# First loads reordered, one product moved into the drain, and tokens 2p and 2p+1 to a partition, in a two-layer transformer kernel

## The chip, the cores and the metric

The kernel runs on one core of a Trainium2 chip. A core has five engines with instruction queues of their own: TensorE (PE in the profile, with its weight loads as PEld), VectorE (DVE), ScalarE (ACT), GpSimd (POOL) and SyncE (SP), which here issues nearly all DMAs. The metric is the device time of one launch in microseconds (us); less is better.

## The reference, cut to what matters

The input x is 16 sequences (batches) of 256 tokens by 256 features, in fp32. Four residual steps follow each other:

```python
x = x + attn0(cond(x, fside, fside, braak_embed[itok_5]))     # 16 heads of 16, causal, rotary
x = x + ffn0(cat_linear(x, W[itok_63], b[itok_63]))           # fp4-quantized gate, up, down
x = x + attn1(du_dt(x, zX, zY, zR))                           # 16 heads of 64, segments of 128
x = x + moe(partly_shared_mlp(x, experts[itok_15]))           # 8 experts, top 2, one shared
```

The first argument of `attn0` is itself an attention over `fside`, with one row of an embedding added to the queries. `du_dt`, which the change touches, is a reaction and diffusion step with reflecting borders, along the features and along the tokens:

```python
lap_x = y[:, :, left] - 2*y + y[:, :, right]     # neighbouring features
lap_y = y[:, up, :]   - 2*y + y[:, down, :]      # neighbouring tokens
du_dt = zX*lap_x + zY*lap_y + zR*y*(1 - y)
```

The fourth step first applies a 256 to 1024 layer with Gelu (`fc1`), then a 1024 to 192 layer that all sequences share (`fc2`) beside a 1024 to 64 layer chosen by the sequence; a router then sends each token to two of eight experts.

## The kernel before, in words

All products are fp32 on TensorE. In the trace each fp32 product is two MATMUL records, and each transpose (a product with the identity) one; the fillers are two.

The first stage, `woven`, does the first three steps for the 16 batches in a software pipeline. Eleven generators (`stage_a`, `stage_e`, `stage_gate`, `stage_up`, `stage_down`, `stage_f`, `stage_g`, `stage_p`, `stage_d`, `stage_v`, `stage_fill`) each yield one instruction at a time, or a condition to wait for. `weave` picks, while the program is built, the instruction that can start first by its own cost table, so the order on each engine is fixed in the program, by estimates in which every load takes 4.5 us. PSUM is split into two pairs of banks (`pair0`, `pair1`) and four `single` banks, handed out by the same list. All these instructions appear under one line (L162) in the profile.

`stage_a` loads batch 0 by `fetch_a`, then the weights of the first attention, and computes the cross attention and the heads' projections; `stage_gate`, `stage_up` and `stage_down` meanwhile load the feed-forward weights as `raw` tiles (`f_v` for the up matrix), quantize them and transpose them. `stage_fill` puts products of the identity on PE until the first batch has passed the first attention. `stage_e` finishes that attention, `stage_f` is the feed-forward step, `stage_p` loads the tables of the second attention and projects, `stage_d` calls `diffuse` (du_dt and the normalization), and `stage_g` and `stage_v` are the scores and the values of the second attention. `stage_v` ends each batch by storing x to a DRAM tensor `xd[b]`.

x is held as two tiles of 128 tokens: partition p holds tokens p and 128 + p. In `diffuse` the token neighbours come from a product with a 256 by 256 matrix `lap` (tridiagonal with the reflecting border), two products of K = 128 for each of the two token halves.

Near the end of the first stage, after the last batch has passed the feed-forward step, `stage_e` releases the memory of the first attention and calls `fetch_c`, which loads `x0` (batches 0 and 1 from `xd`), `fc1`, `fc2` and other weights of the fourth step ahead of it.

The second stage, `mixture`, begins with `conditioned`: for each of 8 blocks of 512 tokens it transposes x, multiplies by `fc1` with Gelu into `hT` (from a pool `k.hp` with two buffers), multiplies by `fc2` and by the chosen expert's matrix `own`, and routes. The shared expert and the tiles of the routed experts follow, then a gather that combines.

The queue of SP is served in order. `row_of` and `fetch_f` read an index of the batch from the tile `idx` on SP before they issue a load, so SP stands there until `idx` has landed.

Of the kernel before, what the change touches and what calls it, by code (L numbers as in the profile page):

```python
# [12 lines left out]
F32 = mybir.dt.float32  # L13
# [49 lines left out]
def setup(ctx, tc, a, n_batch):  # L63
    nc = tc.nc
    k = Ctx()
    k.nc, k.tc, k.a, k.B, k.turn, k.stream = nc, tc, a, n_batch, False, 0
    k.const = ctx.enter_context(tc.tile_pool(name="const", bufs=1))
    c = k.const
    k.ident = c.tile([P, P], F32, name="ident")
    make_identity(nc, k.ident)  # L70

    k.mask = c.tile([P, P], F32, name="mask")
    make_causal_mask(nc, k.mask, mask_val=NEG)


    idx = c.tile([64, 3, n_batch], I32, name="idx")
    for i, name in enumerate(("itok_B_0_5", "itok_B_0_63", "itok_B_0_15")):
        nc.sync.dma_start(out=idx[:, i, :], in_=a[name].unsqueeze(0).to_broadcast([64, n_batch]))
    k.idx = idx
    idxf = c.tile([64, 3, n_batch], F32, name="idxf")  # L80
    nc.vector.tensor_copy(idxf, idx)
    iota = c.tile([64, 1], F32, name="iota")
    nc.sync.dma_start(out=iota, in_=a["iota"])
    k.onehot = c.tile([64, 3, n_batch], F32, name="onehot")
    nc.vector.tensor_scalar(k.onehot, idxf, iota, None, ALU.is_equal)


    k.n_tiles = (TOPK * n_batch * S + NE * (TT - 1)) // TT
    dram = ctx.enter_context(tc.tile_pool(name="dram", bufs=1, space=bass.MemoryType.DRAM))
    k.ysort = dram.tile([NE * REGION * TT, D], F32, name="ysort")  # L90
    k.osort = dram.tile([k.n_tiles * TT, D], F32, name="osort")
    k.zero = c.tile([P, D], F32, name="zero")
    nc.gpsimd.memset(k.zero, 0.0)

    k.xd = [dram.tile([S, D], F32, name=f"xd{b}") for b in range(n_batch)]
    return k
# [198 lines left out]
def woven(k):  # L295
    nc, tc = k.nc, k.tc
    with ExitStack() as ctx:
        g = Stages()
        g.k, g.a, g.B, g.ident = k, k.a, k.B, k.ident
        g.pe, g.dve, g.act = Unit("PE", nc.tensor), Unit("DVE", nc.vector), Unit("ACT", nc.scalar)  # L300
        g.pool, g.sp = Unit("POOL", nc.gpsimd), Unit("SP", nc.sync)
        pool = lambda name, bufs, **kw: ctx.enter_context(tc.tile_pool(name=name, bufs=bufs, **kw))
        g.w = pool("w", 1)
        g.xp = pool("x", 5)
        g.f_, g.l_ = pool("sf", 1), pool("sl", 1)

        g.attention0 = tc.tile_pool(name="sa", bufs=1, side="right")
        g.a_ = g.attention0.__enter__()
        space = bass.MemoryType.PSUM
        psum = pool("psum", 1, space=space)  # L310
        g.pairs = [psum.tile([P, 2, 512], F32, name=f"pair{i}") for i in range(PAIRS)]
        g.singles = [psum.tile([P, 512], F32, name=f"single{i}") for i in range(8 - 2 * PAIRS)]
        g.zT = {}
        g.live, g.kT = {}, {}
        g.x, g.io, g.done = {}, {}, {"W": 0, "D": 0, "Z": 0, "A": 0, "M": 0, "E": 0, "F": 0, "P": 0, "G": 0, "V": 0, "L": 0}
        with tc.manual_schedule():
            weave([stage_a(g), stage_e(g), stage_gate(g), stage_up(g), stage_down(g), stage_f(g), stage_g(g), stage_p(g), stage_d(g), stage_v(g), stage_fill(g)])
# [41 lines left out]
def stage_a(g):  # L359
    k, a = g.k, g.a  # L360
    yield from fetch_a(g, 0)
    g.bout, op = load(g, g.w, "bout0", [P, D], a["L0_attn_b_out"].unsqueeze(0).to_broadcast([P, D]))
    yield op
# [4 lines left out]
    for name in ("cos0", "sin0", "nsin0"):  # L368
        t, op = load(g, g.w, name, [P, 2, DH0 // 2], a[name])
        setattr(g, name, t)  # L370
        yield op
    g.wout0, op = load(g, g.w, "wout0", [P, 2, D], a["w_out0"])
# [10 lines left out]
    for b in range(g.B):  # L383
        x = g.x[b]
        yield g.pool.tensor_tensor(x, x, g.bout.unsqueeze(1).to_broadcast([P, 2, D]), ALU.add)
        hT = yield from cross_attention(g, b)
        if b + 1 < g.B:
            yield lambda: b + 1 < g.done["L"] + 5
            yield from fetch_a(g, b + 1)
        yield lambda: g.done["A"] == b  # L390
        yield from project_heads(g, hT)
        for n in range(4):
            yield lambda: 4 * b + n < g.done["E"] + 2
            g.kT[4 * b + n] = yield from heads_maximum(g, n)
            g.done["M"] += 1


def stage_e(g):

    for b in range(g.B):  # L400
# [19 lines left out]
        yield copy_(g, oT, pt)  # L420
# [13 lines left out]
def fetch_c(g):  # L434

    k, a = g.k, g.a
    k.c2 = k.tc.tile_pool(name="c2_w", bufs=1, side="right")
    w = k.c2.__enter__()
    k.early = {}
# [12 lines left out]
    yield from get("fc2b", [P, 1], a["fc2_b"][0:P].unsqueeze(1))  # L452
    yield from get("wr", [P, 2, P + NE])
    yield g.sp.dma_start(out=k.early["wr"][:, :, P:], in_=a["w_router"])
    yield from get("expb", [16, 64], a["L1_cond2_experts_b"])
    yield from get("shared_b", [64, 1], a["fc2_b"][P : P + 64].unsqueeze(1))
# [3 lines left out]
    yield from get("bias2", [P, g.B])  # L460
    yield from get("xT0", [P, 2, 512])


def fetch_a(g, b):
# [9 lines left out]
    yield g.sp.dma_start(out=fT, in_=a["fT"][b])  # L474
    yield g.sp.dma_start(out=e, in_=row_of(g, a["L0_cond_braak_embed"], 0, b))
    yield g.sp.dma_start(out=f, in_=a["fside_BxSxS_0"][b].rearrange("(c p) d -> p c d", p=P))
    yield g.sp.dma_start(out=g.x[b], in_=a["x"][b].rearrange("(c p) d -> p c d", p=P))
# [173 lines left out]
def stage_f(g):  # L651
    k, a = g.k, g.a
    g.wc = {}
    yield from fetch_f(g, 0)
# [84 lines left out]
def quant_rows(g, name, dst, raw_tile, scratch):  # L739

    for r in range(0, FF0, 2 * P):
# [3 lines left out]
        for i in range(2):  # L745
            n = min(P, FF0 - r - i * P)
            yield g.sp.dma_start(out=raw[:n, i, :], in_=g.a[name][r + i * P : r + i * P + n, :])
        if both:
            flat = raw.rearrange("p i d -> p (i d)")
            yield from quantize(g, flat, flat, 2 * D, P, scratch)  # L750
        else:
            yield from quantize(g, raw[:, 0, :], raw[:, 0, :], D, P, scratch)
            yield from quantize(g, raw[:rows, 1, :], raw[:rows, 1, :], D, rows, scratch)
# [26 lines left out]
def stage_down(g):  # L780
# [3 lines left out]
    for r in range(2):  # L784
        raw = g.f_.tile([P, FF0], F32, name="raw", tag="d_h")
        yield g.sp.dma_start(out=raw, in_=g.a["L0_ffn_w_down"][r * P : (r + 1) * P, :])
        yield from quantize(g, raw, raw, FF0, P, scratch)
# [61 lines left out]
def stage_p(g):  # L849
    k, a = g.k, g.a  # L850
    yield lambda: g.done["A"] > 0 and g.done["W"] == 3
    g.lap, op = load(g, g.w, "lap", [P, 2, S], a["lap"])
    yield op
    g.z = []
    for n in ("condB_zX", "condB_zY", "condB_zR"):
        t, op = load(g, g.w, n, [P, g.B], a[n].unsqueeze(0).to_broadcast([P, g.B]))
        g.z.append(t)
        yield op
    g.gn, op = load(g, g.w, "g", [P, 2], a["g"])
# [61 lines left out]
def diffuse(g, b):  # L921

    zx, zy, zr = (z[:, b : b + 1] for z in g.z)
    y = g.x[b]
    one = yield from single(g, y)
    ply = one.rearrange("p (s d) -> p s d", s=2)
    for st in range(2):
        yield from mm_(g, ply[:, st, :], [(g.lap[:, c, st * P : (st + 1) * P], y[:, c, :]) for c in range(2)])
# [4 lines left out]
    yield g.dve.tensor_scalar(u, y, -1.0, 1.0, ALU.mult, ALU.add)  # L933
    yield g.dve.scalar_tensor_tensor(u, y, zr, u, ALU.mult, ALU.mult)
    yield g.dve.scalar_tensor_tensor(lx, y, -2.0, lx, ALU.mult, ALU.add)
# [16 lines left out]
    for c in range(2):  # L952
        yield g.act.activation(zT[:, c, :], pt[:, c, :], AF.Copy, scale=g.gn[:, c : c + 1])
# [49 lines left out]
def stage_v(g):  # L1003

    for i in range(4 * g.B):
# [4 lines left out]
        if n == 3:  # L1010
            yield g.sp.dma_start(out=g.k.xd[b].rearrange("(s p) d -> p s d", p=P), in_=g.x.pop(b))
            g.done["L"] = b + 1
# [37 lines left out]
def values4(g, n, b, prob, pm, v, wo):  # L1050
# [20 lines left out]
    yield copy_(g, oT, po)  # L1071
    g.singles.append(one)
    if n % 2 == 1:
# [5 lines left out]
        yield copy_(g, ppT, pt)  # L1079
# [16 lines left out]
def mixture(k, out):  # L1096
# [5 lines left out]
    with ExitStack() as ctx:  # L1102
# [6 lines left out]
        k.hp = ctx.enter_context(tc.tile_pool(name="moe_h", bufs=2))  # L1109
# [40 lines left out]
def shared_block(k, r, w1, w2, blk):  # L1150

    nc = k.nc
    hT = k.hp.tile([P, 8, 512], F32, name="hT", tag="hT")
# [250 lines left out]
def conditioned(k, keep, r):  # L1404
# [3 lines left out]
    with ExitStack() as ctx:  # L1408
        p2 = ctx.enter_context(tc.tile_pool(name="c2_p2", bufs=2))
        fc1, fc1b, fc2, fc2b, wr = (k.early[n] for n in ("fc1", "fc1b", "fc2", "fc2b", "wr"))  # L1410
        own = [k.early[f"own{i}"] for i in range(2)]

        nc.vector.tensor_copy(wr[:, :, 0:P], k.ident.unsqueeze(1).to_broadcast([P, 2, P]))

        bias2 = k.early["bias2"]
        nc.vector.tensor_copy(bias2[0:64, :], k.early["shared_b"].to_broadcast([64, B]))
        pb = bank(k)
        mm(nc, pb[64:128, :B], [(k.early["expb"], k.onehot[0:16, 2, :])])
        nc.vector.tensor_copy(bias2[64:128, :], pb[64:128, :B])

        for blk in range(NT // 4):
            k.stream = blk % 2
            for b in (2 * blk, 2 * blk + 1):
# [6 lines left out]
            xT = p2.tile([P, 2, 512], F32, name="g_xT", tag="g_xT", bufs=1) if blk % 2 else k.early["xT0"]  # L1430
            xs = k.xs[:, 4 * blk : 4 * blk + 4, :] if blk else k.early["x0"]
            transposed(
                k,
                xT.rearrange("p c (s t) -> p (c s) t", t=P),
                [xs[:, s, c * P : (c + 1) * P] for c in range(2) for s in range(4)],
            )
            x = k.xs[:, 4 * blk : 4 * blk + 4, :]
            nc.gpsimd.tensor_tensor(x, x, k.bs2.unsqueeze(1).to_broadcast([P, 4, D]), ALU.add)
            hT = k.hp.tile([P, 8, 512], F32, name="hT", tag="hT")
            for f in range(8):  # L1440
# [5 lines left out]
            nc.vector.tensor_scalar(k.yT[:, 0, blk * 512 : (blk + 1) * 512], py, fc2b, None, ALU.add)  # L1446
            for i in range(2):
# [22 lines left out]
def program(tc, a, out, n_batch):  # L1470
    with ExitStack() as ctx:
        k = setup(ctx, tc, a, n_batch)
        woven(k)
        mixture(k, out)

# [97 lines left out]
```

## Time and profile before

| | |
|---|---|
| median of 3 runs | 2772.08 us (2769.31 to 2772.41) |
| profiled execution, its own time | 2774.55 us |
| its span, first to last instruction | 2772.9 us |
| PE, PEld busy | 2692.8, 2039.9 us |
| DVE, ACT, POOL busy | 1434.2, 935.5, 858.2 us |
| mean granted TensorE clock | 0.983 |
| DMA | 270.65 MB, mean 98 GB/s |

Busy time is the union of an engine's instructions. In the page's strips the span is cut into 40 slices of 69 us; a digit is the busy share in tenths. A line of a timeline gives the start, the duration, the engine, the kernel's line, the operation and its tiles as out<-in, how many were merged, and in brackets the idle time before it and what ended it. A line of the stretches gives the busy time of PE, PEld, DVE, ACT and POOL with the number of instructions, then the granted clock, the busy share of the DMA engines and GB/s.

The first stage ends near 1795 us, where the last x is stored. The conditioned blocks reach to about 2070 us, the experts to 2657 us.

### The profile page before, as it was taken

What the parts mean: (1) busy time and instruction counts of PE and PEld (TensorE: products, weight loads), DVE (VectorE), ACT (ScalarE), POOL (GpSimd) and SP (SyncE); (2) the same over time, 40 slices, a digit from 0 to 9 for tenths busy, and PEclk for the clock granted to TensorE, in tenths of its full rate; (3) what the DMA queues carried; (4) which work ended last, traced back from release to release, by engine and by line L of the source; (5) the groups of instructions that cost most, each with busy time, mean ns of one, the idle gap of its engine ahead of it and who ended that gap; (6) DMA issues with size and microseconds to landing.
All of it is one profiled execution on the core that took longest, in us unless ns stands there. A gap on an engine that the chain in (4) does not pass through costs nothing. (4 is left out here: it accounts for less than half of the span.)

```text
span 2772.9 us, 42339 instructions
## 1 busy us (share of the span) xinstructions
PE 2692.8 (97%) x15999; PEld 2039.9 (74%) x15999; DVE 1434.2 (52%) x3113; ACT 935.5 (34%) x2418; POOL 858.2 (31%) x1030
## 2 busy tenths in 40 slices
PE   7999999999999999999999999899999999999999
PEld 6666777777777777777777778655566888888866
DVE  6556676776776776776776776433340000000023
ACT  2323334333333333333333334332222222222221
POOL 4323344434434334434434443323320000000035
PEclk7989999999999999999999999999999999999999
DMA  3222132222222222222322223131111455555523
GB/s 114 58 65 92 46 97 72 85 81 68 90 76 69 94 73 71 94 73 68 97 73 67 77 87 124 56 116 52 50 45 70 149 191 197 187 194 199 198 86 107
DMA packets 196030, 270.65 MB, mean 98 GB/s; under 512 B 33904, under 2 KB 166768, under 8 KB 186480
## 3 DMA queue, kind: packets, MB, share of 16 engines
q1 hardware_dynamic: 189680, 251.13, 28.2%
q0 software_dynamic: 6144, 16.79, 1.9%
q8 instruction: 128, 2.10, 0.3%
q14 instruction: 78, 0.64, 0.1%
HBM read 207.31 MB, written 60.56 MB: 97 GB/s over the span
## 5 line engine op out<-in xcount | busy, mean ns | idle before, releaser
L162 ACT ACTIVATE f_prob<-pair,f_stat 128x144 f32<-128x144 f32 x512 | 190.7, 378 | 225.8 <-DVE f_stat L162 172.0
L162 DVE TENSOR_TENSOR pair<-pair,mask 128x256 f32<-128x256 f32 (+1 forms) x384 | 198.5, 517 | 124.2 <-PE pair L162 92.8
L1228 POOL DMA_INDIRECT got<-osort,pos_o x64 | 62.0, 969 | 626.8 <-ACT hT L1161 586.3
L1210 ACT ACTIVATE ehT<-bank,own_b 128x256 f32<-128x256 f32 x280 | 132.8, 474 | 348.8 <-PE bank L49 348.8
L162 PE MATMUL single<-e_zT,wq 128*128 128x256 f32 x1024 | 249.6, 387 | 0.0
L49 PE MATMUL bank<-ysT,w 128*128 128x256 f32 x1120 | 247.6, 379 | 0.2 <-ACT ysT L113 0.2
L49 PE MATMUL bank<-w,ehT 128*128 128x256 f32 x1120 | 247.5, 379 | 0.0
L49 PEld LDWEIGHTS bank<-ysT,w 128*128 128x128 f32 x1120 | 212.7, 190 | 29.4 <-ACT ysT L113 0.5
L49 PEld LDWEIGHTS bank<-w,ehT 128*128 128x128 f32 x1120 | 210.2, 190 | 27.2
L162 PEld LDWEIGHTS single<-e_zT,wq 128*128 128x128 f32 x1024 | 186.8, 191 | 33.6 <-issue 4.5
L162 PE MATMUL pair<-keys,f_q 32*128 32x144 f32 x2048 | 159.8, 294 | 0.2 <-ACT f_prob L162 0.2
L162 ACT ACTIVATE b_e<-pair 128x768 f32<-128x768 f32 x128 | 103.7, 810 | 161.5 <-PE pair L162 151.4
L162 PEld LDWEIGHTS pair<-keys,f_q 32*128 32x128 f32 x2048 | 132.4, 184 | 27.7 <-issue 22.8
L162 POOL TENSOR_SCALAR_AFFINE_SELECT b_e<-b_e 128x512 f32<-128x512 f32 x128 | 83.9, 656 | 211.1 <-ACT b_e L162 210.3
L1218 DVE TENSOR_TENSOR eo<-bank,eb 128x512 f32<-128x512 f32 x35 | 24.2, 692 | 234.4 <-PE bank L49 227.8
L162 POOL TENSOR_TENSOR keys<-f_t,f_t 128x256 f32<-128x256 f32 x128 | 94.8, 754 | 150.9 <-DVE f_t L162 146.5
L162 PE MATMUL single<-wo,f_oT 128*128 128x256 f32 x512 | 131.9, 391 | 8.9 <-ACT f_oT L162 8.6
L162 DVE TENSOR_REDUCE qpad<-pair 128x2 f32<-128x256 f32 (+1 forms) x256 | 131.0, 554 | 4.4
L162 DVE TENSOR_TENSOR x<-x,single 128x512 f32<-128x512 f32 (+1 forms) x112 | 67.6, 604 | 121.2 <-PE single L162 121.1
L162 PE MATMUL pair<-b_qkT 16*128 16x128 f32 (+1 forms) x1024 | 123.3, 362 | 4.7 <-ACT b_qkT L162 3.3
L162 POOL TENSOR_TENSOR f_q<-f_t,f_t 128x256 f32<-128x256 f32 x128 | 93.5, 751 | 110.0 <-DVE f_t L162 109.7
L162 POOL TENSOR_TENSOR f_prob<-f_prob,f_stat 128x1024 f32<-128x1024 f32 x64 | 125.9, 1967 | 0.0
(300 smaller groups left out, 5240.0 us busy)
## 6 DMA issues: line engine op xcount, KB each, us to landing
w<-in_w SPq DMA_DIRECT2D x70, 1024.0 KB
ysort<-zero SPq DMA_DIRECT2D x32, 1024.0 KB
wq<-in_w_qk SPq DMA_DIRECT2D x128, 256.0 KB
wv<-in_w_v SPq DMA_DIRECT2D x64, 256.0 KB
wo<-in_w_out SPq DMA_DIRECT2D x64, 256.0 KB
ys<-ysort SPq DMA_DIRECT2D x35, 256.0 KB
osort<-eo SPq DMA_DIRECT2D x35, 256.0 KB
eb<-in_b SPq DMA_DIRECT2D x35, 128.0 KB
```

The lines of the kernel that those rows point to most:

```text
L49: nc.tensor.matmul(out, lhsT, rhs, start=start and i == 0, stop=stop and i == last)
L162: return Op([(self.name, self.cost(fn, outs, aps), lambda: call(*args, **kw))], outs, aps)
L1210: nc.scalar.activation(hT[:, f, :], ph, AF.Gelu_apprx_tanh, bias=b1[:, f : f + 1])
L1218: nc.vector.tensor_tensor(o, po, b2.unsqueeze(1).to_broadcast([P, 2, D]), ALU.add)
L1228: nc.gpsimd.indirect_dma_start(out=g, out_offset=None, in_=k.osort[:, :], in_offset=bass.IndirectOffsetOnAxis(ap=r.pos_o[:, i, t : t + 1], ...
```

## The change

Four things are changed together.

1. Loads. The three index loads leave `setup`; `fetch_a` issues them for batch 0 behind xT and fT and then lets SP wait until the first `raw` loads of the gate, up and down matrices have been issued (`done["R"] == 3`) before the embedding row, f and x. The bias `bout` is loaded behind the rotary tables, and added to x after the cross attention instead of before it. `stage_f` makes its first load after `wout0` has been issued. The one-hot of the third index (of 16 rows, in place of 64 rows of three) is made in `stage_p`.
2. Drain. A new stream `stage_c` starts when the last scores have been issued: it transposes x0 and does `fc1` and Gelu of block 0 into a tile `hT0` that is allocated by `fetch_c`. `conditioned` skips these for block 0. Even blocks keep `hT0`, odd blocks the one buffer left in `k.hp`. Small loads (`expb`, `fc2_b`) move from `fetch_c` to `conditioned`, and the bias product of the experts behind `fc2` of block 0.
3. Tokens. Partition p of x holds tokens 2p and 2p+1, so a load or a store of x is one run of 2 KB in each partition. Where a product's columns were in token order (`oT`, `f_oT`, `f_ppT`, `zT`), the copy out of PSUM now reads, or for `zT` writes, every second element.
4. Laplacian. With neighbours 2p and 2p+1 in one partition, the token neighbours of one parity are all in the other, so `diffuse` needs one product of K = 128 for each half, with a two-band matrix that POOL builds from the identity. The terms in y itself are folded into a factor: u = y*(zc - zR*y), zc = zR - 2*(zX + zY), which takes one VectorE instruction less.

The diff, cut to its core:

```diff
@@ setup
-    for i, name in enumerate(("itok_B_0_5", "itok_B_0_63", "itok_B_0_15")):
-        nc.sync.dma_start(out=idx[:, i, :], in_=a[name].unsqueeze(0).to_broadcast([64, n_batch]))
...
+    k.idx = c.tile([64, 3, n_batch], I32, name="idx")
+    k.onehot = c.tile([16, n_batch], F32, name="onehot")
@@ stage_a
     yield from fetch_a(g, 0)
-    g.bout, op = load(g, g.w, "bout0", [P, D], a["L0_attn_b_out"].unsqueeze(0).to_broadcast([P, D]))
-    yield op
...
+    g.bout, op = load(g, g.w, "bout0", [P, D], a["L0_attn_b_out"].unsqueeze(0).to_broadcast([P, D]))
+    yield op
     g.wout0, op = load(g, g.w, "wout0", [P, 2, D], a["w_out0"])
...
     for b in range(g.B):
+        hT = yield from cross_attention(g, b)
         x = g.x[b]
         yield g.pool.tensor_tensor(x, x, g.bout.unsqueeze(1).to_broadcast([P, 2, D]), ALU.add)
-        hT = yield from cross_attention(g, b)
@@ stage_e
-        yield copy_(g, oT, pt)
+        yield copy_(g, twined(oT), untwined(pt))
@@ fetch_c
+    k.h0 = k.tc.tile_pool(name="moe_h0", bufs=1, side="right")
+    hT0 = k.h0.__enter__().tile([P, 8, 512], F32, name="hT0")
...
+    g.done["C"] = 1
+
+def stage_c(g):
+    yield lambda: g.done["C"] and g.done["G"] == 4 * g.B
+    e = g.k.early
+    x, xT = e["x0"], e["xT0"]
+    for c in range(2):
+        one = yield from single(g, x)
+        pt = one.rearrange("p (s t) -> p s t", t=P)
+        for s in range(4):
+            yield g.pe.transpose(pt[:, s, :], x[:, s, c * P : (c + 1) * P], g.ident)
+        yield copy_(g, xT[:, c, :], one)
+        g.singles.append(one)
+    for f in range(8):
+        one = yield from single(g, xT)
+        yield from mm_(g, one, [(e["fc1"][:, c, f * P : (f + 1) * P], xT[:, c, :]) for c in range(2)])
+        yield g.act.activation(e["hT0"][:, f, :], one, AF.Gelu, bias=e["fc1b"][:, f : f + 1])
+        g.singles.append(one)
+
+def hidden(k, blk):
+    return k.early["hT0"] if blk % 2 == 0 else k.hp.tile([P, 8, 512], F32, name="hT", tag="hT")
+
+def untwined(t):
+    return t.rearrange("p c (t r) -> p c r t", r=2)
+
+def twined(t):
+    return t.rearrange("p c (r t) -> p c r t", r=2)
@@ fetch_a
     yield g.sp.dma_start(out=fT, in_=a["fT"][b])
+    if b == 0:
+        for i, name in enumerate(("itok_B_0_5", "itok_B_0_63", "itok_B_0_15")):
+            yield g.sp.dma_start(out=g.k.idx[:, i, :], in_=a[name].unsqueeze(0).to_broadcast([64, g.B]))
+        yield lambda: g.done["R"] == 3
     yield g.sp.dma_start(out=e, in_=row_of(g, a["L0_cond_braak_embed"], 0, b))
...
-    yield g.sp.dma_start(out=g.x[b], in_=a["x"][b].rearrange("(c p) d -> p c d", p=P))
+    yield g.sp.dma_start(out=g.x[b], in_=a["x"][b].rearrange("(p c) d -> p c d", p=P))
@@ stage_f
+    yield lambda: hasattr(g, "wout0")
     yield from fetch_f(g, 0)
@@ quant_rows, stage_down: behind the raw loads of a round
+        g.done["R"] += r == 0
@@ stage_p
-    g.lap, op = load(g, g.w, "lap", [P, 2, S], a["lap"])
-    yield op
+    g.lap, one = g.w.tile([P, 2, P], F32, name="lap"), g.ident
+    for r, dst, end in ((0, 1, 0), (1, 0, P - 1)):
+        cols = g.lap[:, r, dst : dst + P - 1]
+        yield g.pool.tensor_tensor(cols, one[:, 0 : P - 1], one[:, 1:P], ALU.add)
+        yield g.pool.tensor_tensor(g.lap[:, r, end : end + 1], one[:, end : end + 1], one[:, end : end + 1], ALU.add)
...
+    yield g.dve.tensor_tensor(zc, g.z[0], g.z[1], ALU.add)
+    yield g.dve.scalar_tensor_tensor(zc, zc, -2.0, g.z[2], ALU.mult, ALU.add)
+    yield g.dve.tensor_scalar(g.z[2], g.z[2], -1.0, None, ALU.mult)
@@ diffuse
     for st in range(2):
-        yield from mm_(g, ply[:, st, :], [(g.lap[:, c, st * P : (st + 1) * P], y[:, c, :]) for c in range(2)])
+        yield g.pe.matmul(ply[:, st, :], g.lap[:, st, :], y[:, 1 - st, :], start=True, stop=True)
...
-    yield g.dve.tensor_scalar(u, y, -1.0, 1.0, ALU.mult, ALU.add)
-    yield g.dve.scalar_tensor_tensor(u, y, zr, u, ALU.mult, ALU.mult)
-    yield g.dve.scalar_tensor_tensor(lx, y, -2.0, lx, ALU.mult, ALU.add)
+    yield g.dve.tensor_scalar(u, y, nzr, zc, ALU.mult, ALU.add)
+    yield g.dve.tensor_tensor(u, y, u, ALU.mult)
     yield g.dve.scalar_tensor_tensor(u, lx, zx, u, ALU.mult, ALU.add)
     yield g.dve.scalar_tensor_tensor(u, ply, zy, u, ALU.mult, ALU.add)
...
-        yield g.act.activation(zT[:, c, :], pt[:, c, :], AF.Copy, scale=g.gn[:, c : c + 1])
+        by_token = zT[:, c, :].rearrange("p (t r) -> p r t", r=2)
+        yield g.act.activation(by_token, pt[:, c, :].rearrange("p (r t) -> p r t", r=2), AF.Copy, scale=g.gn[:, c : c + 1])
@@ values4
-    yield copy_(g, oT, po)
+    yield copy_(g, twined(oT), untwined(po))
...
-        yield copy_(g, ppT, pt)
+        rows = lambda t: t.unsqueeze(1)
+        yield copy_(g, twined(rows(ppT)), untwined(rows(pt)))
@@ conditioned
+            hT = hidden(k, blk)
+            for f in range(8 if blk else 0):
```

## The prediction

> **What bounds the kernel now.** I read the page first, then the busy time by stretch, the groups of instructions, and the timelines of the two ends of the first stage.
>
> ```profile
> span 2772.9 us, 42339 instructions
> ...
> PE 2692.8 (97%) x15999; PEld 2039.9 (74%) x15999; DVE 1434.2 (52%) x3113; ACT 935.5 (34%) x2418; POOL 858.2 (31%) x1030
> ...
> PE   7999999999999999999999999899999999999999
> ...
> PEclk7989999999999999999999999999999999999999
> ```
>
> TensorE is busy 97% of the span; of the 40 slices only the first (7) and the 26th (8) are lower. So time is won by giving TensorE less work, or by filling those two holes. By stretch (PE, PEld, DVE, ACT and POOL busy, granted clock, DMA share, GB/s):
>
> ```profile
> 0.00:10.00 10.00, 7.96 (x52) 7.77 (x52) 0.63 (x2) 1.28 (x1) 4.30 (x14) 1.00 0.36 92
> 10.00:20.00 10.00, 2.84 (x7) 2.31 (x8) 0.98 (x3) 0.00 (x0) 2.48 (x2) 0.62 0.85 264
> 20.00:30.00 10.00, 6.42 (x36) 5.37 (x35) 9.76 (x19) 3.92 (x9) 6.62 (x8) 0.84 0.42 144
> 800.00:1200.00 400.00, 392.90 (x2813) 297.30 (x2810) 290.10 (x589) 157.78 (x454) 159.89 (x195) 1.00 0.25 79
> ```
>
> In the middle PE is idle 7.1 us of 400 and DVE is 73% busy. The first 10 us of PE are filler products; at 10 to 20 nothing computes while DMA moves 264 GB/s; at 20 to 30 DVE is full, with the quantization of the weights. The start in time order (start, duration, what, idle before and its releaser):
>
> ```profile
> 13.03 1.80 SPq L162 DMA_DIRECT2D raw<-in_L_ffn_w_gate  x2
> 14.62 1.26 POOL L162 TENSOR_TENSOR x<-x,bout 128x512 f32<-128x512 f32 x1 [9.54 <-DMA bout<-in_L_attn_b_out]
> 15.84 1.26 POOL L162 TENSOR_TENSOR a_qT<-xT,emb 128x512 f32<-128x512 f32 x1
> 17.16 3.78 PE L162 MATMUL pair<-fT,a_qT 128*128 128x256 f32 x8 [7.64 <-POOL a_qT L162]
> 18.95 0.69 DVE L162 TENSOR_REDUCE q_amax<-raw 128x32 f32<-128x512 f32 x1 [13.59 <-DMA raw<-in_L_ffn_w_gate]
> 23.65 0.68 DVE L162 TENSOR_REDUCE a_stat<-pair 128x2 f32<-128x512 f32 x1
> ```
>
> POOL waits for the bias `bout`, DVE for the first weight rows: both are late because they were issued late. The end of the first stage:
>
> ```profile
> 1777.72 1.99 PE L162 MATMUL single<-wo,f_oT 128*128 128x256 f32 x8
> ...
> 1782.83 1.90 POOL L162 TENSOR_TENSOR f_prob<-f_prob,f_stat 128x1024 f32<-128x1024 f32 x1
> ...
> 1784.78 1.97 PE L162 MATMUL single<-ident,f_prob 128*128 128x128 f32 x8 [5.06 <-POOL f_prob L162]
> ...
> 1797.23 14.00 PE L49 MATMUL bank<-xT,fc 128*128 128x512 f32 x32 [0.28 <-ACT xT L113]
> ...
> 1811.07 7.03 PE L49 MATMUL bank<-hT,fc 128*128 128x512 f32 x16
> ```
>
> PE stands 5.06 us behind the last softmax; the granted clock is then 0.50 from 1786 to 1794, so the last chain runs at half speed. The 14.00 us of `xT,fc` need nothing of that chain.
>
> **The change, part by part.** All durations are of the profiled execution: span 2772.9, its own time 2774.55, which is 2.5 above the median 2772.08. I take the differences off the median.
>
> Start. The program of the changed kernel has the same order on PE, DVE and ACT for the first 70 rows or so; only SP moves. It issues xT, fT, three idx, two raw gate, two f_v, raw down, then emb. Ahead of emb stand 256+256+12+256+256+352 KB. The DMA moved 190 to 260 GB/s in most stretches of this start and 362 at best, so with its own 128 KB emb needs 4 to 8 us from the first traffic, which comes about 1 us after the first issue at 0.8. Its own issue comes at about 6.5 (from 0.8 on: seven issues of 0.4, three of 0.6, and 0.8 for reading idx, as at 5.5 to 6.29 now). I estimate the landing at 10 (9 to 12). Then a_qT 1.26, no longer behind x+bout 1.26; scores 2.0 to 3.8 by the clock (1.99 in the middle of the run, 3.78 here); a_stat at about 15 instead of 23.65. The other way to a_stat: raw gate lands near 8, three rounds of amax, unit, reciprocal on DVE take 4.5, q_xn behind a_qT ends near 12.4, ACT 0.63, and q_big comes near 13.3: earlier. So -8.5; ends -4 (emb at 13 and a cold clock) and -10. Moved past on SP: the 1.5 MB now stand ahead of f, x, wqkv and bqkv. wqkv is then about 2.9 MB deep, landing at 11 to 15; it was first used at 33.41 and will be wanted at 25, so this is covered. bout now lands last and x+bout stands on POOL behind quantization work, wanted only at the residual sum at 98 us.
>
> Laplacian. 64 of 128 records `single<-x,lap` go. Eight of them take 1.83 us of PE from start to start (1081.91 to 1083.74), so four take 0.915; times 16 batches 14.6 us. PE is the bound in all but the first; I take -14. Ends: -15.25 (half of the group's 30.5 us busy) and -8, if the batches fall back on their chains. On DVE `lx-2y` (750 ns) goes and an 819 ns form becomes a plain product (nearest 604 to 690): 16 x 0.9 = 14 us off an engine that is 73% busy, counted at nothing. POOL builds the bands with four instructions (0.43 to 0.51 each by f_pm and e_lx), and DVE gets five of 0.2 near 98 us, where it idled 1.9 us before b_qk. They wait for zX, zY, zR and iota; if those land late, b_qk and the projection behind it wait. The lap load of 256 KB ahead of them is gone; 0, ends 0 and +2.
>
> Order of small products. Two 16 or 17 row groups that stand next to each other on PE save time: `b_qkT` and `b_qS` take 0.85 each alone, 1.51 together on the same rows (1059.11 to 1060.62), 0.88 together on other rows (1048.66 to 1049.54); so 0.2 or 0.83 saved. The program has 27 neighbours on other rows and 40 on the same before, 25 and 61 after (the keys groups behave alike, 1.18 alone): 30.4 against 33.0 us, -2.5; ends 0 and -4.
>
> x+bout behind the cross attention. PE waits 12.4 us for a_qT in 13 places, 7.6 of it at the start; the other 4.8 can fall by up to the 1.3 of x+bout each: -2, ends 0 and -4.8.
>
> Tokens 2p, 2p+1. Loads and stores of x become one run of 2 KB in place of two of 1 KB: DMA is at 0.25, 0. The copies f_oT (64), b_oT (16), f_ppT (32) read PSUM, and e_zT (32) writes SBUF, at every second element. No row shows that from PSUM; on SBUF the strided `b_t<-b_qk,sin` takes 432 ns against 415 for vpad, 4% more. I take 0 by that row; below 0 there is no reason. The upper end is doubled time for each element: ACT 586 for 512 and 373 for 256 gives 0.83 ns, so +0.43 and +0.21: 64x0.43 + 16x0.43 + 64x0.21 = 48 us on engines a third busy. PE waited for f_oT 13 times of 64, so about a quarter shows: +12.
>
> Drain. From 1779.7 the new order on PE is: x0 transposes 1.1, end 1780.8; xT copies behind the exps on ACT (1782.15) to 1783.35; fc1 0 in 1.75 to 1784.8; then f_prob, fc1 1, f_prob (1.1 and 1.75, end 1787.8, no 5 us hole, so no half clock), fc1 2, f_pT, fc1 3, f_pm, fc1 4 (5.25 and 1.4, end 1794.5), wo and pmo 2.9, fc1 5 to 7 in 5.25: 1802.6. The first bank then waits for the last Gelu of the old pool, 1.1: 1803.7 against 1811.07, -7.3. Behind the late x sum, SP stores xd and loads the rest of xs about 2 us later than now; block 1 wants them near 1819 and they land before 1810. Ends -4 (Gelus, behind one table load of 1.28, hold up the singles) and -9.
>
> Sum: -8.5 -14 -2.5 -2 -7.3 = -34.3; 2772.1 - 34.3 = 2738.
>
> [...]
>
> **The rivals.**
> Dear strided copies, which end on the other side. Place: f_oT, between values and output product, 64 times, and the three others. At double element time it decides against the change once 34.3 of the 48 us (71%) show on PE: at all of it 2738+48 = 2786, at a quarter 2750. For: PE already waits 8.6 us for f_oT. Against: 51 of 64 copies have slack, and SBUF's row is 4%. Chance 0.07, 0.03 of it slower. [...]
> Lost start. The early stretch fits no simple bound: clock 0.50 at 50 to 67, 132 to 152 and 190 to 203 us. If DVE and emb give only 4 and the half-clock stretches, 82 us before 310, grow by 8 (4 us of PE), 2738+4.5+4 = 2746 or so. Chance 0.15.
> Chains, not PE. Then the Laplacian gives 4 of 14 and the order 0: 2750. For: PEld is 74%, and a modelled PE can look full. Against: start to start of neighbours shows no gap. Chance 0.10.
> The change does not do what it says: the loads land no earlier, since the same bytes share the same engines (0 at the start), the Gelus of the drain hold up the singles and give back its 7.3, and the batches fall back on their chains. Then -4 from the Laplacian and -2 from POOL are left: 2766. For: DMA is already at 264 GB/s in the hole. Against: from 0 to 5 us it moves next to nothing. Chance 0.03.
>
> **How the numbers follow.** Forecast 0.65, 2738, own range 2726 to 2748. The range takes in the lost start, the chains and a quarter of dear copies, and downwards all best ends but one (-43, 2729) with clock stretches that vanish: 2723 to 2760. About 0.2% (5.5 us) is what a measurement here can tell from no change. Slower: 0.03 of the copies and 0.01 of the last rival. The same: 0.01 of the copies and 0.02 of the last. Faster: the rest, 0.93.
>
> **What would show it.** Right: a_stat near 15; 64 records of `x,lap` of the same length; no 5 us hole and no half clock at the drain; first `hT,fc` 7 us closer to the last f_prob product; f_oT at 586. Wrong: f_oT near 1000 and PE waits for it well over 8.6 us; a_qT still at 15; more time at half clock before 310 us; an idle PE in the middle above 7.1 us of 400.

## The result, and the profile after

| | before | changed |
|---|---|---|
| median of 16 runs | 2774.17 us (2769.31 to 2781.92) | 2765.66 us (2761.38 to 2773.94) |
| ratio | | 0.9966, 95% interval 0.9958 to 0.9974 |
| profiled span | 2772.9 us | 2767.1 us |
| PE, PEld busy | 2692.8, 2039.9 us | 2687.6, 2028.2 us |
| DVE, ACT, POOL busy | 1434.2, 935.5, 858.2 us | 1411.4, 945.9, 863.7 us |

The kernel became faster by 0.34%, some 9 us, where 34 were forecast. The page of the changed kernel, the lines that answer to those of before:

```profile
span 2767.1 us, 42187 instructions
...
PE 2687.6 (97%) x15929; PEld 2028.2 (73%) x15929; DVE 1411.4 (51%) x3061; ACT 945.9 (34%) x2457; POOL 863.7 (31%) x1034
...
PE   8999999999999999999999999999999999999999
...
PEclk7889999999999999999999999999999999999999
```

Both low slices of the PE strip have filled: the first went from 7 to 8, the 26th from 8 to 9. Yet PE is at 97% as before. By stretch, with the columns explained above:

```profile
10.00:20.00 10.00, 6.90 (x29) 6.18 (x30) 4.88 (x10) 2.96 (x7) 7.13 (x8) 0.66 0.89 310
20.00:30.00 10.00, 6.95 (x33) 4.49 (x32) 9.62 (x14) 2.82 (x6) 7.26 (x6) 1.00 0.33 109
800.00:1200.00 400.00, 391.05 (x2792) 294.47 (x2792) 282.25 (x569) 159.22 (x463) 162.25 (x195) 1.00 0.24 77
```

At 10 to 20 us PE now computes, and the DMA engines move 310 GB/s instead of 264. In the middle PE is *less* busy: 391.05 us of 400 against 392.90, so 9.0 us idle against 7.1, with 21 records fewer in the stretch. This is where the expected gain is missing, and the prediction had named it as a sign of being wrong (more than 7.1 us idle of 400). It is seen best in the distance between two batches, here two successive groups of the products with `lap` on PE, first of the kernel before, then of the changed one:

```profile
977.35 1.89 PE L162 MATMUL single<-x,lap 128*128 128x256 f32 x8
...
1081.91 1.89 PE L162 MATMUL single<-x,lap 128*128 128x256 f32 x8
```

```profile
972.46 1.13 PE L153 MATMUL single<-x,lap 128*128 128x256 f32 x4
...
1077.70 1.13 PE L153 MATMUL single<-x,lap 128*128 128x256 f32 x4
```

Half of the records are gone, as forecast, but the batch takes 105.24 us instead of 104.56. Measured over batches 4 to 12 (start of the first `lap` product of batch 12 less that of batch 4, by 8) the period is 104.55 before and 105.24 after. I use this number, the *period*, for every kernel below: kernels that have the same order and work agree in it within 0.05 us (105.24, 105.23, 105.23 and 105.28 for four), where whole runs of one kernel differ by 10. The period covers these eight batches alone; the first and the last batches have to be read beside it.

The drain, in order of time on PE of the changed kernel:

```profile
1778.35 1.99 PE L153 MATMUL single<-wo,f_oT 128*128 128x256 f32 x8
1780.18 1.04 PE L153 MATMUL single<-ident,x 128*128 128x128 f32 x8
1783.30 3.59 PE L153 MATMUL single<-xT,fc 128*128 128x512 f32 x4 [2.08 <-ACT xT L153]
1786.68 0.74 PE L153 MATMUL single<-ident,f_prob 128*128 128x128 f32 x4
...
1804.69 7.13 PE L49 MATMUL bank<-hT,fc 128*128 128x512 f32 x16 [0.78 <-ACT hT L153]
```

From the group `wo,f_oT` to the first product with `hT` it takes 26.34 us, before 33.35 (1777.72 to 1811.07). The 5.06 us hole has become one of 2.08.

### The profile page after: what moved, and what is told of

It reads as the page before. It is cut to its first block, busy times and chain, and to the rows that moved or that the text cites. A ratio compares the mean times of both kernels' runs of the same rounds, so it can differ in the third digit from the quotient of the medians.

```text
span 2767.1 us, 42187 instructions
## 1 busy us (share of the span) xinstructions
PE 2687.6 (97%) x15929; PEld 2028.2 (73%) x15929; DVE 1411.4 (51%) x3061; ACT 945.9 (34%) x2457; POOL 863.7 (31%) x1034
## 5 line engine op out<-in xcount | busy, mean ns | idle before, releaser
L153 PE MATMUL single<-wv,e_zT 128*128 128x256 f32 x512 | 124.4, 386 | 0.1
```

What stands on the lines that cost most here:

```text
L153: return Op([(self.name, self.cost(fn, outs, aps), lambda: call(*args, **kw))], outs, aps)
```

## The experiments

All times are medians of 4 to 12 runs, ratios are to the kernel before measured beside them. The medians were measured in several sets, in which the kernel before had 2772.8 to 2776.1, so a difference of two medians carries a doubt of some 3 us.

| kernel | what it is | us | ratio (95%) | period |
|---|---|---|---|---|
| old_list | new Laplacian and tokens, order of before | 2769.08 | 0.9990 (0.9977 to 1.0004) | 103.93 |
| rewoven | the same, order woven anew | 2775.64 | 1.0006 (0.9995 to 1.0017) | 104.16 |
| rewoven_bout | the same, x + bout moved | 2775.05 | 0.9995 (0.9985 to 1.0006) | 105.28 |
| loads_bout | the same, loads of the start moved | 2770.14 | 0.9980 (0.9969 to 0.9991) | 105.23 |
| changed_again | the same, new drain: the changed kernel | 2764.90 | 0.9968 (0.9956 to 0.9980) | 105.23 |
| after_bout_first | changed, x + bout back | 2764.61 | 0.9954 (0.9937 to 0.9971) | 104.17 |
| doubled | changed, lap products issued twice | 2769.23 | 0.9992 (0.9979 to 1.0005) | 105.29 |
| swapped | changed, two POOL instructions exchanged | 2757.83 | 0.9940 (0.9922 to 0.9958) | 104.19 |
| old_drain | old_list with the new drain | 2762.82 | 0.9947 (0.9927 to 0.9967) | 103.94 |
| spared | changed, order as if lap were unchanged | 2762.20 | 0.9945 (0.9922 to 0.9968) | 103.96 |
| hoisted | spared, first store of x later on SP | 2756.73 | 0.9928 (0.9910 to 0.9947) | 103.98 |
| hoisted2 | spared, second store of x later on SP | 2750.81 | 0.9904 (0.9887 to 0.9921) | 103.99 |

### The work and the order, taken apart

An edit that changes `weave`'s list reshuffles what stands behind it. To take the work away without that, an `Op` (one entry of the list) can keep its place and its cost in the list and issue something else, or nothing:

```diff
+def stands_for(op, *calls):
+    op.choices = [(name, cost, lambda: [c() for c in calls]) for name, cost, _ in op.choices]
+    return op
@@ diffuse, in the kernel before
-        yield from mm_(g, ply[:, st, :], [(g.lap[...], y[:, c, :]) for c in range(2)])
+        for c in range(2):
+            op = g.pe.matmul(ply[:, st, :], g.lap[...], y[:, c, :], start=c == 0, stop=c == 1)
+            real = lambda st=st: nc.tensor.matmul(ply[:, st, :], g.near[:, st, :], y[:, 1 - st, :], start=True, stop=True)
+            yield stands_for(op, *([real] if c == 0 else []))
```

> The kernel before with the new placement of tokens and the one-product Laplacian, but with the order of every instruction as it was before: the list still sees two products for each half and the third VectorE operation, and only one product and two operations are issued for them. Loads and drain are as before. Theory L (PE's work was worth what the prediction said; the newly woven order took it back): the batch period falls from 104.55 to 103.6 or 103.7 us, 16 batches give -12 to -14, total near 2760, ratio 0.995. Theory C (the waits hold the period whatever the order is, and PE only looks full): the period stays above 104.2, total within 5 us of before, ratio 0.998 or more.

> The same two parts put into the kernel before, with the order woven anew; loads and drain as before. Theory L: the period is 104.5 to 105.3 us, as in the changed kernel (105.24), total 2770 to 2785, that is 8 us or more above the kernel with the old order, though the work is the same. Theory C: within 3 us of the kernel with the old order.

> The changed kernel, whose list still sees a second product for each half of the Laplacian and a third VectorE operation that are not issued. Loads, drain and work are those of the changed kernel; only the order is another. Theory L: period 103.6 to 103.7, start -7 and drain -6.5 as measured, total 2745 to 2749, ratio 0.990 to 0.991. Theory C: the same as the changed kernel, 2762 to 2768, ratio 0.9966.

> The changed kernel in its own order, with each product of the Laplacian issued twice (the second repeats the first), 64 records more. Theory L (in any one order PE's work counts nearly in full): +10 to +14 us, total 2776 to 2780, ratio 1.0005 to 1.002. Theory C (in the new order waits are the bound and cover PE's work): +4 us at most, total 2766 to 2770, ratio 0.997 to 0.9985.

(The third VectorE operation is treated in the same way.) For `doubled` the edit only makes the call of the product twice.

Measured: in the old order the period falls to 103.93, by 0.62, between the two theories. The table of steps (start of each PE record to the start of the next, summed over a batch) shows it exactly: the products of the Laplacian go from 1.82 to 0.96, -0.86; nothing else changes but one group, `b_e,vpad`, which goes from 3.15 to 3.45, +0.30 (the rest is -0.06). So PE's work counts, less what the next wait takes back. The total lies where theory C put it: 4.5 us below before by the medians, and not clear of no change by the ratio. From the first `lap` product to that of batch 15 the trace gains 5.9 us where 15 times 0.62 would be 9.3; most of the rest goes at two holes that before doesn't have (1.96 us at 354.97 and 1.97 at 1600.85, last section).

The same work in the newly woven order gives 104.16, and 1757.6 instead of 1748.3 us at the first `wo,f_oT` product of the last batch: 9.3 us later in the two profiled executions, 6.6 by the medians, with more time at half clock (mean granted clock 0.981 in the profiled execution of rewoven, 0.983 in that of old_list). This is the way theory L points, but not its numbers (a period of 104.5 to 105.3, 8 us or more). `spared` shows that the period can be had back: 103.96. But its median stayed 13 us above its forecast, at the edge of theory C's range; a part of that has a cause of its own, below.

`doubled` is the sharpest: 64 products more move the period by 0.05. In the steps of a batch the Laplacian is at 1.83 again (+0.86), and `b_e,vpad` falls from 4.18 to 3.40 (-0.78). In the changed kernel's order the saved work had become waiting in front of that one group. The total is less clear than the period: +3.6 us by the medians, but 0.9992 against 0.9966 by the ratios, some 7 us, between the two theories. By the traces `doubled` is 3.0 us behind changed_again at batch 4 and 3.5 at batch 15, so it loses this ahead of the steady loop and next to nothing in it.

### Which edit chose the order

```diff
@@ stage_a, rewoven -> rewoven_bout; after_bout_first is the reverse in the changed kernel
-        yield g.pool.tensor_tensor(x, x, g.bout.unsqueeze(1).to_broadcast([P, 2, D]), ALU.add)
         hT = yield from cross_attention(g, b)
+        x = g.x[b]
+        yield g.pool.tensor_tensor(x, x, g.bout.unsqueeze(1).to_broadcast([P, 2, D]), ALU.add)
```

> The kernel rewoven (before, with the new tokens and the one-product Laplacian, order woven anew) and one thing more: x + bout stands behind the cross attention, as in the changed kernel. Same work, loads and drain as in rewoven. Theory O (the place of that one POOL instruction sends the planner onto another order, and the order sets the batch period): the period is that of the changed kernel, 105.2 us, against 104.16 in rewoven, +9.5 us over nine batches, of which the two last batches give back some 6; total 2775 to 2782. Theory P (the period of the changed kernel comes from the loads or the drain, or from the freed POOL time): the period stays at 104.2, or falls by the up to 1.3 us that a_qT waited.

> The changed kernel with x + bout put back ahead of the cross attention; everything else, the load of bout behind the rotary tables too, as changed. Theory O: the period is that of rewoven, 104.16 instead of 105.24, 9 batches -9.7; the two last batches take some 7 more, as in rewoven; a_qT of batch 0 now waits for the late bout, +2 or +3 at the start: total within 4 us of the changed kernel, 2762 to 2770, with the period as the mark. Theory P: the period stays at 105.2.

Measured: 105.28 with the addition behind the cross attention, 104.17 with it ahead, whatever loads and drain do. Theory O holds for the period: the place of one instruction of 1.27 us on POOL, which was counted as a gain of 2 us, chose an order whose batch is 1.1 us longer. In after_bout_first the start falls back as well (a_stat at 24.4 us instead of 16.9), further than the 2 or 3 us expected. The totals of rewoven and rewoven_bout agree all the same (2775.64 and 2775.05), because that order is 10 us ahead at batch 4 (first `lap` product at 550.8 against 560.8) and quicker over the last two batches (169.9 against 176.9 us from batch 13 to 15).

### What holds PE in that order

POOL and PE of the changed kernel at one place in a batch:

```profile
976.14 0.85 POOL L153 TENSOR_TENSOR f_pm<-f_prob,f_stat 128x128 f32<-128x128 f32 x1
976.95 1.89 POOL L153 TENSOR_TENSOR f_prob<-f_prob,f_stat 128x1024 f32<-128x1024 f32 x1
...
978.44 0.63 PE L153 MATMUL single<-b_e,vpad 128*32 128x256 f32 x4
978.80 0.63 POOL L153 TENSOR_SCALAR_AFFINE_SELECT b_e<-b_e 128x512 f32<-128x512 f32 x1
...
979.49 0.84 PE L153 MATMUL single<-b_e,vpad 128*32 128x256 f32 x12 [0.42 <-POOL b_e L153]
```

PE has issued four of the 16 products `b_e,vpad` and stands for the select of the rest of `b_e`, which waits on POOL behind 1.89 us of `f_prob`. The group takes 1.82 us from start to start instead of 0.79. The gap in the record shows only 0.42 of the 1.03, because the records of the four products before it reach into the wait. The next kernel only exchanges the two on POOL:

```diff
@@ weave, where an instruction is issued
+        if held and engine == "POOL" and out.startswith("b_e"):
+            call()                       # the select first
+            return held.pop()[1]()       # then the multiplication of f_prob
...
+        if engine == "POOL" and out.startswith("f_prob") and "f_stat" in names(op.ins)[-1]:
+            held.append((out, call))
+        else:
+            call()
```

> The changed kernel with one exchange on POOL, twice in a batch: where the multiplication of f_prob (1.9 us) stands directly ahead of a select of b_e, the select goes first. PE, VectorE and ScalarE keep their order, and no work is added or taken. In the changed kernel the first of these places holds the 16 products b_e,vpad for 1.03 us a batch, 0.42 of it shown as a gap. Theory W (that wait is on the path that sets the period): the period falls from 105.24 to 104.2 to 104.6, total -6 to -9, near 2757. Theory M (the wait is only where the slack of another path becomes visible, and it moves): f_prob, now 0.65 later, holds its transposes instead, the period stays above 105.0, total within 2 us.

The same place in this kernel:

```profile
968.84 0.63 POOL L153 TENSOR_SCALAR_AFFINE_SELECT b_e<-b_e 128x512 f32<-128x512 f32 x1
969.44 1.89 POOL L153 TENSOR_TENSOR f_prob<-f_prob,f_stat 128x1024 f32<-128x1024 f32 x1
...
970.35 0.86 PE L153 MATMUL single<-b_e,vpad 128*32 128x256 f32 x16
```

All 16 products run in one go, the period is 104.19, -1.05, and in the steps of a batch `b_e,vpad` falls by 1.03 while no other group moves by more than 0.02. Theory W holds: this wait was on the path. The total falls to 2757.83, ratio 0.9940 against the changed kernel's 0.9966 and 0.9968, so 7 to 8 us (5 to 6.5 if each median is taken less that of before beside it).

The same table closes the account of the period from before to changed, +0.69: the Laplacian's products -0.85, `b_e,vpad` +1.03 (3.15 to 4.18), all other groups together +0.51. In the kernel before this group takes the same 3.15 as in swapped, so the wait was not there. It came in two parts: with the products of the Laplacian doubled the new order has 3.40, and the other 0.78 came as that work was taken away. So the new order costs 0.74 us a batch at the old work (104.55 to 105.29), and in it the saving is worth 0.05.

### The start and the drain

loads_bout is the changed kernel without the drain's part (`stage_c`, `hT0` and the moved small loads); its PE, DVE, ACT and POOL have the order of rewoven_bout up to the last scores, but for two small VectorE instructions that the one-hot needs.

> The changed kernel without the new drain: same order on PE, VectorE, ScalarE and POOL as in rewoven_bout and the changed kernel up to the last scores; against rewoven_bout only the loads of the start differ. Theory S (the start is worth its 7 us, but a half-clock stretch between 46 and 80 us, which comes in two lengths, takes it back in some executions): a_stat near 17, the first product with lap 7 us earlier than in rewoven_bout (near 171) where that stretch is short and about as early (179) where it is 20 us long; median -3 to -7 against rewoven_bout's 2775, that is 2768 to 2772. Rival (the start's gain is lost behind the next wait in every execution): 2775 and the first product with lap at 179 with a short stretch too.

> The changed kernel once more, on the chip of loads_bout. Against loads_bout only the drain differs: -6 to -7 us if the drain keeps what it gained in old_drain, -3 or less if not. The ratio to the kernel before stays within 0.995 to 0.998.

> old_list (the new Laplacian and tokens in the order of before) and the new drain: block 0's first product in the list behind the last scores, nothing else. Theory D (the drain is worth what the prediction says, whatever the rest): everything up to 1745 us as in old_list, the first product with hT 7 us earlier, no half-clock stretch of 10 us behind it, total -6 to -7 against old_list, near 2762. If the gain at the drain needs the other parts: -3 or less.

Measured, start: a_stat (the first reduction of the cross attention's scores) at 18.0 instead of 23.4 us, the first `lap` product at 171.3 instead of 178.5, ratio 0.9980 against 0.9995: theory S. In the profiled execution of the changed kernel the lead of 6.5 us at a_stat was gone by the a_stat of batch 1, at 81.4 us against 80.5 in rewoven_bout. The changed kernel, and then changed_again, by stretch:

```profile
50.00:60.00 10.00, 9.38 (x60) 7.82 (x58) 8.62 (x22) 2.81 (x5) 4.66 (x8) 0.65 0.01 2
60.00:70.00 10.00, 10.00 (x58) 6.82 (x54) 6.41 (x13) 2.02 (x5) 3.17 (x4) 0.50 0.00 0
70.00:80.00 10.00, 10.00 (x70) 8.07 (x69) 4.28 (x9) 4.12 (x9) 3.86 (x4) 0.67 0.01 2
```

```profile
50.00:60.00 10.00, 9.30 (x56) 7.74 (x56) 7.90 (x20) 2.92 (x6) 4.61 (x9) 0.66 0.01 2
60.00:70.00 10.00, 9.87 (x102) 7.60 (x106) 7.93 (x19) 4.83 (x11) 5.24 (x7) 1.00 0.01 2
70.00:80.00 10.00, 9.54 (x92) 7.23 (x85) 5.68 (x13) 4.66 (x13) 3.19 (x5) 1.00 0.15 40
```

The same program in the same order: at 60 to 70 us it is granted 0.50 in one execution and issues 58 records, and 1.00 in the other and issues 102. The half-clock stretch lasts 20.5 us in the first (from 53.0) and 6.8 in the second; the first `lap` product comes at 179.5 and at 172.2. What the loads gain is as large as what this stretch takes or leaves, and the two are not quite separated: of the 7.2 us by which loads_bout leads at the first `lap` product, 4.3 are left from batch 3 on, and it also has 10.2 us less at half clock before 310 us than rewoven_bout (68.3 against 78.5), which at half speed would be worth 5.

Measured, drain: `old_drain` has its first product with `hT` 5.1 us earlier than old_list, though its last batch was 1.8 us later: -6.9 from there, and medians -6.3. In the changed order, changed_again against loads_bout, the medians give -5.2, and the time from the `wo,f_oT` group to the first product with `hT`, read as in the first section, falls from 31.2 to 26.3. By the ratios the drain would be worth 12 us in the old order (0.9947 against 0.9990) and 3.3 in the new (0.9968 against 0.9980); with intervals of 3 to 6 us each, these scatter by as much as is to be measured. By medians and traces it is worth 5 to 7 us in both orders.

### A load behind a store

`spared` lost a part of its forecast at one place. PE and SP there:

```profile
479.74 0.33 SPq L153 DMA_DIRECT2D xd<-x  x1
...
484.02 1.21 SPq L153 DMA_DIRECT2D wq<-in_w_qk  x2
...
489.65 2.93 PE L153 MATMUL single<-e_zT,wq 128*128 128x256 f32 x6 [5.10 <-DMA wq<-in_w_qk]
```

SP stood from 459.9 to 479.7 for x, which the store `xd` writes out; `wq` was issued behind it, and PE idled 5.10 us. The clock was at 0.50 for 6.8 us behind that.

```diff
@@ weave, on SP alone, at one store of x
+        if engine == "SP" and not done and (held or out.startswith("xd1")):   # hoisted: xd0
+            if out[:2] in ("wq", "wv"):                                       # hoisted: wo too
+                call()                                # the weights at once
+                if out[:2] == "wv": done.append(1); [h() for h in held]
+            else: held.append(call)                   # the store and the loads behind it
```

> spared, with one stretch of SP's queue in another order: the first store of x and the loads of batch 5 stand behind the weights (wq, wo, wv) of the next head group instead of ahead of them. In spared PE stood 5.1 us at 484 us for wq, whose load stood behind that store on SP, and a half-clock stretch of 6.8 us followed. Theory H (the late load and the clock cost 5.1 + 3.4): the hole goes, no half clock at 489, total -8 against spared's profiled 2762, near 2754. Rival: the wait moves to batch 5's x or to the store and the total stays within 2 us.

> spared with the swap on SP's queue at the right place: the second store of x, the loads of batch 6 and wo stand behind wq and wv of the next head group. (hoisted made it at the first store, where PE does not wait.) Theory H: the hole of about 5 us at 481 to 490 us and the half clock behind it go, -6 to -8 against hoisted (median 2756.7), near 2750, ratio 0.990 to 0.991. Rival: wq is still late, or a later load takes its place: -2 or less.

Measured: `hoisted` was a miss. I had taken the store of batch 0, and the hole is at that of batch 1: it stayed (4.8 us at 481), and the 5 us in the median go with a shorter half-clock stretch at the start (from 54.3 us 6.8 us long in its profiled execution, from 52.1 us 23.9 long in that of spared), not with the exchange: two of the five runs of spared took 2754.55 and 2755.89, as short as hoisted's. `hoisted2` exchanges at the right store: no gap over 1.5 us between the holes at 355 and 1599, median 2750.81, ratio 0.9904. It is the fastest kernel here, -6 against hoisted as theory H has it; and the profiled executions of spared and hoisted2, which have the same 85.3 us of half clock before 310 us, take 2762.4 and 2755.0. Exchanging the POOL pair in it as well was not tried.

## Why the prediction was wrong

The sum by its own steps, with what the chain rewoven_bout, loads_bout, changed_again gives (ratios times 2775, each with an interval of some 3 us to either side, so that the single rows are rough):

| step | predicted | measured |
|---|---|---|
| start | -8.5 (-4 to -10) | -4.2; by the trace -7.2 at the first `lap` product, -4.3 from batch 3 on |
| Laplacian | -14 (-8 to -15.25) | |
| order of small products | -2.5 (0 to -4) | |
| x + bout | -2 (0 to -4.8) | the three together -1.4 |
| copies | 0 (0 to +12) | 0 |
| drain | -7.3 (-4 to -9) | -3.3; by the traces -4.9 (from loads_bout) to -7.0 (from before) |
| sum | -34.3 | -8.9 |

**The step that failed** is the Laplacian, in its first sentence: "PE is the bound in all but the first". PE was busy 97% and start to start showed no gap between neighbours, so I took each record off PE as its price in time. The work did leave as forecast: 64 records, and 0.85 us a batch by the steps, 13.7 in 16. But a price in time needs more: that the other engines keep PE fed when it needs 0.9 us less, and that the new order is as good as the old. Neither held. Where the order stays, 0.62 of 0.86 us arrive and 0.30 come back as waiting at `b_e,vpad` (old_list), and the total gains 4.5 us by the medians, short of the -8 at which my range for this term ended. Where the order is woven anew, the period falls by 0.39 (rewoven) or rises by 0.73 (rewoven_bout), and in the changed kernel's order the work is worth 0.05 in the period (doubled): a wait for POOL, nearly hidden between overlapping records, is on the path, and swapped takes it away and gets all of it.

The order as a whole was treated as a by-product worth -2.5, counted by neighbours of the same row groups. That count was near: by the steps the three groups (`b_qkT`, `b_qS,b_qkT`, `keys,f_q`) take 0.20 us a batch less, 3.2 in 16. What it left out was larger, and of either sign: at equal work the period is 103.93, 104.16 or 105.28. The sentence on x + bout failed with it: the wait for a_qT did go (12.4 us in 13 places before, 4.4 in one place after, at the start), but the instruction's new place chose another order.

Of the rivals, "Chains, not PE" (0.10) named the mechanism, but gave 4 of 14 and 0 for the order, so 2750; that the order can cost as much as the work saves was in no case, and so the range ended at 2760. The last rival (0.03) gave 2766, the number that came, but by luck: it had the start and the drain give nothing, and both gave. PE's busy share hardly tells the slower order from the faster one: from 800 to 1200 us it is 391.05 us in the changed kernel and 392.03 in swapped. In the one group that differs, 1.03 us of waiting showed as a gap of 0.42, so the records in front of it looked longer than their work.

**Start.** Right in mechanism: emb let a_qT go at 11.79 instead of behind bout at 15.84, a_stat came at 16.9 (predicted 15), the first reduction of the weights on DVE (`q_amax`) at 6.54 instead of 18.95. What the whole run keeps of it goes with the half-clock stretches, as the rival "Lost start" had it: before 310 us they are 82 us in before, and 85 and 68 in two executions of the changed kernel.

**Drain.** Right, and nearest in size: the order on PE is the one written down, 5 to 7 us by the traces. The first fc1 product came at 1783.30 (worked out: 1783.35), but behind its hole of 2.08 us the clock was half for 3.4 us, so it took 3.59 us and not 1.75, and the first `hT,fc` came at 1804.7 (worked out: 1803.7).

**Copies.** Right. The copy of `f_oT` out of PSUM, all of it contiguous before and at every second element after, and `e_zT`, which is written so (least, median and greatest duration in ns):

```profile
L162 ACT COPY f_oT<-single x59: 567/586/596, 278.1 to 1789.2; 128x512 f32<-128x512 f32 x59
L162 DVE COPY f_oT<-single x5: 684/692/692, 362.5 to 1776.7; 128x512 f32<-128x512 f32 x5
...
L162 ACT ACTIVATE e_zT<-single,g x32: 467/474/485, 211.3 to 1676.8; 128x256 f32<-128x256 f32 x32
```

```profile
L153 ACT COPY f_oT<-single x50: 582/586/591, 276.6 to 1792.4; 128x512 f32<-128x512 f32 x50
L153 DVE COPY f_oT<-single x14: 691/692/692, 471.8 to 1777.3; 128x512 f32<-128x512 f32 x14
...
L153 ACT ACTIVATE e_zT<-single,g x32: 478/496/513, 208.0 to 1677.6; 128x256 f32<-128x256 f32 x32
```

586 ns on ACT and 692 on DVE, as before; the write costs 5% more (496 ns against 474). The rival with the dear copies fell: no run shows the doubled element time from which it and the upper end of +12 were reckoned, and for these reads by ACT and DVE the measurement shows no price.

## What to carry to other kernels

In a kernel whose order a planner writes, an edit's price has two parts, the work and the new order; hold the order (an entry that stands for the old one) to see the first alone, and compare periods of the steady loop, which repeat to 0.05 us where runs scatter by 10 (the first and the last batches still need the total: rewoven and rewoven_bout differ by 1.1 us in the period and by 0.6 in the median). A TensorE at 97% did not say here that its work was the time (64 products more moved the period by 0.05 us): issue the products in question twice, and if the period does not move, look at the steps from start to start for the group that waits. There one exchange of two instructions on an engine that is a third busy was worth nearly as much as the whole change.

## What the runs showed of the hardware that was not expected

Short holes cost more than themselves in these runs. Behind a hole of about 2 us on PE the granted clock was 0.50 for 3.4 us in 18 of 34 cases, which at half speed would cost another 1.7 (an estimate: half of 3.4; at the drain of the changed kernel four records `xT,fc` behind such a hole took 3.59 us, and the next four, at 1787.26, 1.88). In old_list, a product behind such a hole, and then the stretch of time that it begins, with the granted clock in the third column from the right:

```profile
354.97 0.66 PE L162 MATMUL single<-ident,c_y 128*128 128x128 f32 x4 [1.96 <-POOL c_y L162]
```

```profile
355.00:359.00 4.00, 3.33 (x10) 1.62 (x10) 2.51 (x5) 1.99 (x7) 2.79 (x2) 0.64 0.00 0
```

A clock of 0.64 over these 4 us, with PE at work for 3.33 of them. The same came at 1601 in old_list, behind 2.0 us at the same products, and in the drain behind 2.08; behind 5.1 us it lasted 6.8 (spared) or 10.2 (before), behind 4.8 in hoisted 3.4. It does not always come: from 300 us on, the 14 profiled executions have 34 holes of 1.9 to 2.1 us, and 18 were followed by it, 16 of the 20 before 1800 us, but only 2 of the 14 near 2650, where every kernel has one. All lengths seen are multiples of 3.41 us (in before and the changed kernel 3.41, 6.83, 10.24, 13.65, 17.07 and 20.48), but for the stretch that the end of the program cuts off (4.54 and 2.57 us). Busy work did not always end it: in the rows above PE is 93 to 100% busy by its records from 50 to 80 us and the clock stays at half for 20.5 us in one execution, for 6.8 in another of the same program. What decides either is open.
